# A two-layer graph network in f32 on one core: layer 0's softmax weights built transposed, head pairs in layer 1, and TensorE in the order in which the program is written

## The chip, the core and the metric

The kernel runs on one core of a Trainium2 chip. The metric is the device time in microseconds of one execution. A core has five engines that run their own instruction queues side by side and wait for each other through semaphores: TensorE (PE; its weight loads are shown as PEld), VectorE (DVE), ScalarE (ACT), GpSimd (POOL) and SyncE (SP), which here issues most of the DMA transfers. The matrix products accumulate in PSUM[...]; all other data lies in SBUF.

## What is computed

64 graphs of 256 nodes with 512 features each go through two layers; each ends in a residual and a layer norm. Layer 0 is graph attention, in 8 heads of 64 units: the score of a pair of nodes is a sum of one number of each node. Layer 1 is ordinary attention whose softmax is mixed with the adjacency matrix. With the node mask (here all ones) left out:

```python
# layer 0
feats   = einsum('bnf,hfu->bhnu', X, W)
e_self  = einsum('bhnu,hu->bhn', feats, a_self)
e_neigh = einsum('bhnu,hu->bhn', feats, a_neigh)
dense   = leaky_relu(e_self[..., :, None] + e_neigh[..., None, :], 0.2)
att     = softmax(dense - 1e10 * (1 - A), axis=-1)
x       = layernorm(X + relu(att @ feats + b))
# layer 1
attn    = 0.33 * softmax(q @ k.T / 8) + 0.33 * A + 0.33 * exp(-A)
x       = layernorm(x + (attn @ v) @ W_out + b_out)
```

## The kernel before

The nodes of a graph stand in two row tiles of 128 (`T`), the features in four chunks of 128 (`C`). A loop over the graphs (line numbers are those of the profile) has two halves. In the first, `attend0(b)` (layer 0's attention) is woven with `proj1(b - 1)` (layer 1's projections of the graph before); in the second, `attend1(b - 1)` with `proj0(b + 1)` (layer 0's projections of the next graph). Each of the four returns a list of thunks, and `together` takes them from the two lists by their counts. The order in which each engine gets its instructions is not this order: the Tile framework's scheduler reorders every engine's instructions by readiness and by its own costs, with the order of writing as the priority.

`proj0` transposes x on TensorE, makes the features (`pf`, L237) and both logits (`pe`, L250), and turns the neighbour logits into rows (`pr`). `attend0` spreads the row of one head over all partitions by a matmul (`pd`, L288), takes the leaky relu on ScalarE (`low`, L292) and VectorE (L300), adds the mask on GpSimd (L308), takes the row maximum on VectorE (L134) and the exponential with its sums on ScalarE (L136). The probabilities are then transposed on TensorE (`pp_h`, L148), copied out of PSUM (L152), and multiplied with the features (`av_h`, L159); a division by the sums follows (L314), then bias (L321), relu with the residual (L325) and the layer norm (L203 to L209, with a square root on ScalarE).

`proj1` makes transposed q and k (`pq`, L385), v (`pv`, L399), and the product of the graph matrix with v (`pcv`, L411, after a transpose of that matrix); a product of the mask with itself (`pm`, L353) gives the mask of the scores. `attend1` takes head by head: scores (`pz`, L438, with 64 rows of the array), the mask added on VectorE (L446), and then the same softmax, transpose and product as layer 0, shared in `heads`. After the division the graph part is added on GpSimd (L459), the output is transposed (`pt_o`, L124) and projected (`po`, L472), and residual, norm and store follow.

[...]SP issues the loads of graph b + 2 at the head of each iteration, and the store of out at its end.

Of the kernel before, what the change touches and what calls it, by code (L numbers as in the profile page):

```python
# [16 lines left out]
def kernel(  # L17
# [18 lines left out]
    T = N // P  # row tiles of one graph  # L36
    C = F // P  # chunks of the feature axis
    HG = H // 2  # heads that share one PSUM bank of outputs
    NEG = 1e10  # layer 0: weight of (adj - 1)
    HIDE = 2.0**100  # layer 1: masked scores; any score is absorbed by it  # L40
    LA = 0.33
    L_BOTH = 0.33  # the weight of the adjacency and of exp(-distance)
# [5 lines left out]
    small = ctx.enter_context(tc.tile_pool(name="small", bufs=4))  # L48
    psum = ctx.enter_context(
# [7 lines left out]
    X, ADJ, MASK = {}, {}, {}  # L57

    def load(b):
        X[b] = io.tile([P, T, F], FT, tag="x", name=f"x_{b}", bufs=3)  # L60
        nc.sync.dma_start(X[b], x[b].rearrange("(t p) f -> p t f", p=P))
        ADJ[b] = io.tile([P, T, N], FT, tag="adj", name=f"adj_{b}", bufs=4)
        nc.sync.dma_start(ADJ[b], adj[b].rearrange("(t p) n -> p t n", p=P))
        MASK[b] = io.tile([1, N], U8, tag="mask", name=f"mask_{b}", bufs=4)
        nc.sync.dma_start(MASK[b], nodemask[b : b + 1, :])
# [4 lines left out]
    w0_sb = consts.tile([P, C, H, U], FT, name="w0_sb")  # L70
    for c in range(C):
        nc.sync.dma_start(
            w0_sb[:, c], w0[:, c * P : (c + 1) * P, :].rearrange("h p u -> p h u")
        )
    a_bc = consts.tile([P, 2, H, U], FT, name="a_bc")
# [9 lines left out]
    # q, k and v columns apart, heads side by side  # L85
# [10 lines left out]
    nc.scalar.dma_start(wo_sb, w_out.rearrange("(c p) f -> p c f", p=P))  # L96

    ident = consts.tile([P, P], FT, name="ident")
    make_identity(nc, ident)
    eps = consts.tile([P, 1], FT, name="eps")  # L100
    nc.vector.memset(eps, EPS)
    # sel[k, h, :] is one where k == h: it spreads row h over all partitions
    sel = consts.tile([H, H, P], FT, name="sel")
    nc.vector.tensor_copy(sel, ident[:H, :H].unsqueeze(2).to_broadcast([H, H, P]))

    # wa[f, 0, h] = sum_u w0[h, f, u] a_self[h, u]; wa[f, 1, h] with a_neigh
    wa = consts.tile([P, C, 2, H], FT, name="wa")
    for c in range(C):
        for s in range(2):
            prod = work.tile([P, H, U], FT, tag="o", name=f"prod_{c}_{s}")  # L110
            nc.vector.tensor_mul(prod, w0_sb[:, c], a_bc[:, s])
            nc.vector.tensor_reduce(wa[:, c, s], prod, AX.X, ALU.add)
    # the scale of the scores goes into q's weights (a power of two)
# [4 lines left out]
    def transposed(src, dst, b, what):  # L118
        """dst[:, c, i] = src[i, c-th feature chunk], one thunk per row tile."""
# [9 lines left out]
        return one  # L129

    def softmax_rows(z, p, ssum, h, b, what):
        """p = exp(z - max over j), ssum its sums; z is [i, t, j]."""
        nmax = small.tile([P, T], FT, tag="nmax", name=f"nmax_{what}_{b}_{h}")
        nc.vector.tensor_reduce(nmax, z, AX.X, ALU.max, negate=True)  # L134
        for t in range(T):
            nc.scalar.activation(  # L136
                p[:, t, :],
                z[:, t, :],
                AF.Exp,
                bias=nmax[:, t : t + 1],  # L140
                accum_out=ssum[:, t, h : h + 1],
            )

    def transpose_probs(p, h, b, what, copy):
        pt = ps_tile([P, T, N], "tr", f"pp_{what}_{b}_{h}")
        for j in range(T):
            for t in range(T):
                nc.tensor.transpose(  # L148
                    pt[:, j, t * P : (t + 1) * P], p[:, t, j * P : (j + 1) * P], ident
                )  # L150
        pT = work.tile([P, T, N], FT, tag="pT", name=f"pT_{what}_{b}_{h}", bufs=3)
        copy(pT, pt)  # L152
        return pT

    def probs_values(av, pT, v, h):
        k = h % HG
        for t in range(T):
            for j in range(T):
                nc.tensor.matmul(  # L159
                    av[:, t, k, :],  # L160
                    pT[:, j, t * P : (t + 1) * P],
                    v[:, j, h * U : (h + 1) * U],
                    start=(j == 0),
                    stop=(j == T - 1),
                )

    def heads(scores, v, rec_scale, done, b, what, copy):
        """Thunks: scores of head h, transposes of head h - 2, values of head h - 3."""
        probs, probsT, av = {}, {}, {}
        ssum = small.tile([P, T, H], FT, tag="ssum", name=f"ssum_{what}_{b}", bufs=2)  # L170
        rec = small.tile([P, T, H], FT, tag="rec", name=f"rec_{what}_{b}", bufs=2)

        def step(i):
# [105 lines left out]
    def attend0(b):  # L279
# [4 lines left out]
        def scores(h):  # L284
            if h == 0:
                nc.vector.tensor_scalar_mul(es5, ECOL[b][:, :, :H], 0.2)
# [283 lines left out]
```

## Time and profile before

| | |
|---|---|
| median of 3 runs | 5749.65 us (5746.13 to 5749.77) |
| profiled execution, span from its first to its last instruction | 5748.6 us |
| mean granted TensorE clock | 0.920 |
| busy: PE, PEld, DVE, ACT, POOL | 96%, 67%, 47%, 47%, 23% |
| DMA | 94.69 MB, mean 16 GB/s |

Times are in microseconds unless marked ns. A row of a group names the line, the engine, the operation, what it writes and what it reads, the shape and the count; behind the first bar stand its total busy time and the mean duration of one in ns, behind the second the idle time of the engine ahead of it and what ended it. A row of the timeline has its start, its length, and the instruction with its count. Matmuls are pipelined and their ends are modelled, so what a matmul costs is read from start to next start. A row of the windows has, for a stretch, the busy time and the count of PE, PEld, DVE, ACT and POOL, then the granted clock, the DMA share and GB/s. A row of the DMA list ends with the size of one transfer and its median time from issue to landing.

### The profile page before, as it was taken

The numbers are of one execution on the slowest core, as the hardware profiler recorded it, in microseconds if no ns is written. First come the engines' busy times: TensorE is split into PE (matmuls) and PEld (weight loads), VectorE is DVE, ScalarE is ACT, GpSimd is POOL, SyncE is SP. The second block draws the span as 40 slices with busy tenths as digits, with TensorE's granted clock in tenths as the row PEclk, the third lists the DMA queues.
The fourth block names the chain that finished last, engine by engine and source line by source line (L and its number), as shares of the span: only waits on it lengthen the run. The fifth ranks groups of instructions, "written<-read, shape, count | busy, mean of one in ns | idle before, by whom it ended". The sixth has DMA issues, their size and how long they took to land.

```text
span 5748.6 us, 70111 instructions
## 1 busy us (share of the span) xinstructions
PE 5528.5 (96%) x26240; PEld 3830.8 (67%) x26240; DVE 2687.0 (47%) x5526; ACT 2712.3 (47%) x7104; POOL 1307.0 (23%) x1350
## 2 busy tenths in 40 slices
PE   7999999999999999999999999999999999999999
PEld 5666666666666666666666666666666666666666
DVE  3444544444444444444444444544444445444444
ACT  4444454454444544444445444454454444544543
POOL 2222222122221222222212222222122222222221
PEclk8999999999999999999999999999999999999998
DMA  2000000000000000000000000000000000000000
GB/s 74 15 14 15 17 15 15 14 19 14 15 15 13 19 16 14 16 17 15 15 14 19 15 14 15 17 15 15 14 19 14 16 15 14 18 15 14 12 8 8
DMA packets 70435, 94.69 MB, mean 16 GB/s; under 512 B 19920, under 2 KB 36304, under 8 KB 70096
## 3 DMA queue, kind: packets, MB, share of 16 engines
q1 hardware_dynamic: 56512, 84.96, 4.5%
q10 hardware_dynamic: 13584, 5.24, 0.4%
q8 instruction: 208, 3.41, 0.2%
q14 instruction: 131, 1.07, 0.1%
HBM read 56.64 MB, written 33.55 MB: 16 GB/s over the span
## 4 chain that ended last, share of the span: by engine, by line
PE 91%; ACT 5%; DVE 2%; POOL 1%; issue 1%; DMA 0%; ACTq 0%; SPq 0%; POOLq 0%; DVEq 0%
PE pq L385 19%; PE av_h L159 16%; PE pp_h L148 10%; PE po L472 9%; PE pz L438 8%; PE pf L237 8%; PE pv L399 8%; PE pd L288 5%; PE pcv L411 4%; PE pe L250 2%; ACT low L292 2%; PE pt_o L124 2%; ACT L206 1%; ACT hT L127 1%; DVE z L446 1%; POOL o L459 1%
## 5 line engine op out<-in xcount | busy, mean ns | idle before, releaser
L136 ACT ACTIVATE p_h<-z,nmax_h 128x256 f32<-128x256 f32 x2048 | 1023.3, 501 | 1146.9 <-DVE nmax_h L134 1135.1
L385 PE MATMUL pq<-hT,wqkv_sb 128*128 128x256 f32 x4096 | 1178.8, 438 | 58.0 <-ACT hT L127 58.0
L385 PEld LDWEIGHTS pq<-hT,wqkv_sb 128*128 128x128 f32 x4096 | 868.9, 224 | 195.5 <-ACT hT L127 83.2
L134 DVE TENSOR_REDUCE nmax_h<-z 128x2 f32<-128x512 f32 x1024 | 695.6, 679 | 586.9 <-POOL z L308 584.8
L308 POOL TENSOR_TENSOR z<-z,m 128x512 f32<-128x512 f32 x512 | 648.9, 1268 | 1006.9 <-DVE z L300 821.2
L148 PEld LDWEIGHTS pp_h<-ident,p_h 128*128 128x128 f32 x4096 | 542.3, 156 | 362.4 <-issue 220.3
L148 PE MATMUL pp_h<-ident,p_h 128*128 128x128 f32 x4096 | 749.4, 299 | 1.9 <-ACT p_h L136 1.9
L300 DVE SCALAR_TENSOR_TENSOR z<-pd,ecol,low 128x256 f32<-128x256 f32 x1024 | 455.2, 476 | 424.5 <-ACT low L292 419.5
L159 PEld LDWEIGHTS av_h<-v,pT_h 128*128 128x128 f32 x4096 | 507.8, 194 | 103.5 <-DVE pT_h L152 52.0
L459 POOL TENSOR_TENSOR o<-o,cv 128x256 f32<-128x256 f32 x256 | 180.3, 726 | 1741.0 <-DVE o L452 1741.0
L159 PE MATMUL av_h<-v,pT_h 128*128 128x64 f32 x4096 | 530.5, 274 | 36.0 <-DVE pT_h L152 36.0
L159 PEld LDWEIGHTS av_h<-feat,pT_h 128*128 128x128 f32 x4096 | 513.9, 194 | 55.7 <-issue 30.8
L292 ACT ACTIVATE low<-pd,es 128x256 f32<-128x256 f32 x1024 | 434.1, 469 | 229.7 <-PE pd L288 221.1
L159 PE MATMUL av_h<-feat,pT_h 128*128 128x64 f32 x4096 | 526.7, 272 | 0.0
L438 PE MATMUL pz<-qk 64*128 64x256 f32 x2048 | 510.3, 404 | 13.5 <-DVE z L446 13.5
L472 PE MATMUL po<-wo_sb,oT 128*128 128x512 f32 x1024 | 517.6, 651 | 0.0
L237 PE MATMUL pf<-w_sb,xT 128*128 128x512 f32 x1024 | 499.8, 605 | 0.0
L399 PE MATMUL pv<-wqkv_sb,hT 128*128 128x512 f32 x1024 | 477.6, 599 | 0.0
L152 DVE COPY pT_h<-pp_h 128x512 f32<-128x512 f32 x512 | 351.5, 686 | 245.6 <-PE pp_h L148 240.1
L446 DVE TENSOR_TENSOR z<-pz,hid 128x512 f32<-128x512 f32 x512 | 345.5, 685 | 176.0 <-PE pz L438 169.2
L479 DVE TENSOR_TENSOR x<-po,x 128x512 f32<-128x512 f32 x128 | 88.6, 692 | 718.7 <-PE po L472 718.7
L152 ACT COPY pT_h<-pp_h 128x512 f32<-128x512 f32 x512 | 300.1, 586 | 215.6 <-PE pp_h L148 213.1
(68 smaller groups left out, 5550.0 us busy)
## 6 DMA issues: line engine op xcount, KB each, us to landing
x<-in_x_dram SPq DMA_DIRECT2D x64, 512.0 KB, 3.5
out_dram<-y SPq DMA_DIRECT2D x64, 512.0 KB, 2.8
adj<-in_adj_dram SPq DMA_DIRECT2D x64, 256.0 KB, 2.6
wqkv_sb<-in_L_gnn_W_qkv_dram ACTq DMA_DIRECT2D x12, 256.0 KB, 6.7
mask<-in_nodemask_dram SPq DMA_DIRECT2D x64, 0.2 KB
w_sb<-in_L_gnn_W_dram SPq DMA_DIRECT2D x4, 256.0 KB, 7.3
wo_sb<-in_L_gnn_W_out_dram ACTq DMA_DIRECT2D x1, 1024.0 KB, 7.3
a_bc<-in_L_gnn_a_self_dram ACTq DMA_DIRECT2D x1, 256.0 KB
```

Source lines behind the costliest of these rows:

```text
L134: nc.vector.tensor_reduce(nmax, z, AX.X, ALU.max, negate=True)
L136: nc.scalar.activation(p[:, t, :], z[:, t, :], AF.Exp, bias=nmax[:, t : t + 1], accum_out=ssum[:, t, h : h + 1],)
L148: nc.tensor.transpose(pt[:, j, t * P : (t + 1) * P], p[:, t, j * P : (j + 1) * P], ident)
L152: copy(pT, pt)
L159: nc.tensor.matmul(av[:, t, k, :], pT[:, j, t * P : (t + 1) * P], v[:, j, h * U : (h + 1) * U], start=(j == 0), stop=(j == T - 1),)
L237: nc.tensor.matmul(pf, xT[:, c, t * P : (t + 1) * P], w0_sb[:, c].rearrange("p h u -> p (h u)"), start=(c == 0), stop=(c == C - 1),)
L292: nc.scalar.activation(low[:, t, :], pd, AF.Identity, bias=es5[:, t, h : h + 1], scale=0.2,)
L308: nc.gpsimd.tensor_add(z, z, M0[b])
L385: nc.tensor.matmul(pq[:, s, :], wqkv_sb[:, c, s, 2 * g : 2 * g + 2, :].rearrange("p h u -> p (h u)"), hT[:, c, :], start=(c == 0), stop=(c ...
L399: nc.tensor.matmul(pv, hT[:, c, t * P : (t + 1) * P], wqkv_sb[:, c, 2].rearrange("p h u -> p (h u)"), start=(c == 0), stop=(c == C - 1),)
L438: nc.tensor.matmul(pz[:, t, :], QK[b][r : r + U, g, 0, t * P : (t + 1) * P], QK[b][r : r + U, g, 1, :], start=True, stop=True,)
L472: nc.tensor.matmul(po, oT[:, c, t * P : (t + 1) * P], wo_sb[:, c, :], start=(c == 0), stop=(c == C - 1),)
```

## The change

Layer 0. A head's weights are made with the neighbour on the partitions, so that they can enter the product without a transpose. For this the row maximum is known beforehand: since leaky relu grows with its argument, the largest neighbour logit among the neighbours (`shifts`, 16 fused add-and-minimum reductions on VectorE) gives it. What is then one number per row becomes, transposed, a row for all partitions: `spread` transposes it on TensorE, copies it, writes it to memory (8 KB) and reads it back to all 128 partitions (1 MB). This is done once for the neighbour logits (`rows`) and, after the shifts, twice for the two branches of the leaky relu with the shift taken off (`rows_ab`). `weights(h)` takes the larger branch, adds the transposed mask on GpSimd and takes one exponential; a column of ones in the features gives the sums. The logits are eight extra columns of the features' product.

Layer 1. The masks are made on GpSimd. Two heads are taken together: the scores on the two row halves of the array, and the values, with v as the stationary operand, on two column halves, which gives the output already transposed. The probabilities are divided by their sums, and the graph matrix is added to them, before the transpose; the product of the graph matrix with v goes away.

Both. The root of the norms is a power on GpSimd. `together` weighs thunks by costs, and TensorE's instructions keep the order of writing. ADJ and the mask have three buffers for four.

```diff
+        nc.gpsimd.tensor_scalar_add(rstd, mv[:, :, 1], EPS)
+        nc.gpsimd.tensor_tensor(rstd, rstd, mhalf, op=ALU.pow)
...
+    def spread(cols, k, tag, b, bufs):
+        pr = ps_tile([k, N], "tr", f"pr_{tag}_{b}")
+        for t in range(T):
+            nc.tensor.transpose(pr[:, t * P : (t + 1) * P], cols[:, t, :k], ident)
+        row = small.tile([k, N], FT, tag=f"row_{tag}", name=f"row_{tag}_{b}", bufs=1)
+        nc.vector.tensor_copy(row, pr)
+        there = dram.tile([k, N], FT, tag=f"there_{tag}", name=f"there_{tag}_{b}")
+        nc.sync.dma_start(there, row)
+        bc = work.tile([P, k, N], FT, tag=f"bc_{tag}", name=f"bc_{tag}_{b}", bufs=bufs)
+        nc.sync.dma_start(bc, there[:, :].partition_broadcast(P))
+        return bc
...
+        def features(t, g):
+            pf = ps_tile([P, W1], "mm", f"pf_{b}_{t}_{g}")
...
+            nc.vector.tensor_copy(ECOL[b][:, t, g, :], pf[:, HG * U :])
+            nc.scalar.copy(
+                feat(b)[:, t, g * HG : (g + 1) * HG, :U],
+                pf[:, : HG * U].rearrange("p (h u) -> p h u", u=U),
+            )
         def rows():
+            n_bc[0] = spread(ECOL[b][:, :, 1, :], H, "n", b, 1)
+        def shifts():
+            nmax = small.tile([P, T, H], FT, tag="nmax", name=f"nmax_{b}", bufs=2)
+            for h in range(H):
+                for t in range(T):
+                    junk = work.tile([P, N], FT, tag="junk", name=f"junk_{b}_{h}_{t}")
+                    nc.vector.tensor_tensor_reduce(
+                        out=junk,
+                        in0=n_bc[0][:, h, :],
+                        in1=m0[:, t, :],
+                        scale=-1.0,
+                        scalar=3.0e38,
+                        op0=ALU.add,
+                        op1=ALU.min,
+                        accum_out=nmax[:, t, h : h + 1],
+                    )
...
+        def rows_ab():
+            for g in range(2):
+                ABC[b, g] = spread(
+                    AB[b][:, :, g].rearrange("p t s h -> p t (s h)"), H, "ab", b, 3
+                )
         return [
+            (0.0, bias),
+            *transposed(X[b], xT, b, "x"),
+            *((1.77, lambda t=t: features(t, 1)) for t in range(T)),
+            (0.22, rows),
+            *((1.77, lambda t=t: features(t, 0)) for t in range(T)),
+            (0.44, bias_T),
+            (0.0, shifts),
+            (0.22, rows_ab),
         ]
...
+        def weights(h):
+            g, k = divmod(h, HG)
+            z = work.tile([P, T, N], FT, tag="z", name=f"z0_{b}_{h}", bufs=4)
             for t in range(T):
                 nc.scalar.activation(
+                    z[:, t, :],
+                    ABC[b, g][:, HG + k, :],
                     AF.Identity,
+                    bias=N5[b][:, t, h : h + 1],
                 )
             for t in range(T):
                 nc.vector.scalar_tensor_tensor(
                     z[:, t, :],
+                    ABC[b, g][:, k, :],
+                    ECOL[b][:, t, 1, h : h + 1],
+                    z[:, t, :],
                     op0=ALU.add,
                     op1=ALU.max,
                 )
+            nc.gpsimd.tensor_add(z, z, M0T[b])
+            nc.scalar.activation(z, z, AF.Exp)
+            E[h] = z
+        def values(h):
+            g, k = divmod(h, HG)
             for t in range(T):
+                if k == 0:
+                    av[g, t] = ps_tile([P, HG, U + 1], "av", f"av0_{b}_{g}_{t}")
+                for j in range(T):
+                    nc.tensor.matmul(
+                        av[g, t][:, k, :],
+                        E[h][:, j, t * P : (t + 1) * P],
+                        feat(b)[:, j, h, :],
...
+        def step(i):
+            if i < H:
+                weights(i)
+            if 0 <= i - 2 < H:
+                values(i - 2)
+        return [
+            (0.9 if i >= 2 else 0.0, lambda i=i: step(i)) for i in range(H + 2)
+        ] + [(0.0, end)]
...
+            *transposed(X1[b], hT, b, "h"),
+            (0.0, masks),
+            *((3.46, lambda g=g: qk(g)) for g in range(G)),
+            *((3.43, lambda t=t: values(t)) for t in range(T)),
...
+        def scores(g):
+            pz = [ps_tile([P, T, N], "sc", f"pz_{b}_{g}_{r}") for r in range(2)]
+            for t in range(T):
+                for r in range(2):
+                    rows = slice(r * U, (r + 1) * U)
+                    nc.tensor.matmul(
+                        pz[r][:, t, :],
+                        QK[b][rows, g, 0, t * P : (t + 1) * P],
+                        QK[b][rows, g, 1, :],
...
+            for r in range(2):
+                h = 2 * g + r
+                z = work.tile([P, T, N], FT, tag="p", name=f"p_{b}_{h}", bufs=5)
+                for t in range(T):
+                    nc.vector.tensor_tensor_reduce(
+                        out=z[:, t, :],
+                        in0=pz[r][:, t, :],
+                        in1=HID[b][:, t, :],
...
+            nc.vector.reciprocal(rec[:, :, s], ssum[:, :, s])
...
+                    nc.vector.scalar_tensor_tensor(
+                        probs[h][:, t, :],
+                        probs[h][:, t, :],
+                        rec[:, t, h : h + 1],
+                        CM[b][:, t, :],
+                        op0=ALU.mult,
+                        op1=ALU.add,
+                    )
...
+        def values(g):
+            if g % 2 == 0:
+                av[g // 2] = ps_tile([P, 2, N], "av", f"av1_{b}_{g}")
+            o = av[g // 2]
+            for j in range(T):
+                for r in range(2):
+                    h = 2 * g + r
+                    nc.tensor.matmul(
+                        o[r * U : (r + 1) * U, g % 2, :],
+                        V[b][:, j, h * U : (h + 1) * U],
+                        probsT[h][:, j, :],
...
+        steps = [(0.0, residual)]
+        for i in range(G + 2):
+            if i < G:
+                steps.append((1.2, lambda i=i: scores(i)))
+            if 0 <= i - 1 < G:
+                steps.append((0.9, lambda i=i: flip(i - 1)))
+            if 0 <= i - 2 < G:
+                steps.append((1.2, lambda i=i: values(i - 2)))
         return [
             *steps,
+            *((3.43, lambda t=t: project(t)) for t in range(T)),
+            (0.0, end),
         ]
...
     def together(one, two):
+        total = [max(sum(c for c, _ in x), 1e-6) for x in (one, two)]
+        done = [0.0, 0.0]
         i = j = 0
+        while i < len(one) or j < len(two):
+            first = j >= len(two) or (
+                i < len(one) and done[0] / total[0] <= done[1] / total[1]
+            )
...
+    with tc.manual_schedule(engines={mybir.EngineType.PE}):
```

## The prediction

> **What bounds the kernel now.** I read the page first: busy shares, the chain that ended last, the costliest groups.
>
> ```profile
> PE 5528.5 (96%) x26240; PEld 3830.8 (67%) x26240; DVE 2687.0 (47%) x5526; ACT 2712.3 (47%) x7104; POOL 1307.0 (23%) x1350
> ...
> PE 91%; ACT 5%; DVE 2%; POOL 1%; issue 1%; DMA 0%; ACTq 0%; SPq 0%; POOLq 0%; DVEq 0%
> ```
>
> TensorE carries 91% of the chain; the others are half idle. So I took TensorE's timeline in one middle graph and read what each piece costs from start to next start, not from its busy time, since matmuls overlap.
>
> ```profile
> 2504.84 3.67 PE L385 MATMUL pq<-hT,wqkv_sb 128*128 128x256 f32 x16
> 2508.44 0.69 PE L288 MATMUL pd<-erow,sel 8*128 8x256 f32 x2
> 2509.06 0.66 PE L148 MATMUL pp_h<-ident,p_h 128*128 128x128 f32 x4
> 2509.56 1.00 PE L159 MATMUL av_h<-feat,pT_h 128*128 128x64 f32 x8
> 2510.40 3.67 PE L385 MATMUL pq<-hT,wqkv_sb 128*128 128x256 f32 x16
> ...
> 2530.35 1.14 PE L438 MATMUL pz<-qk 64*128 64x256 f32 x8
> 2531.42 0.66 PE L124 MATMUL pt_x<-ident,x 128*128 128x128 f32 x4
> ...
> 2538.16 1.13 PE L438 MATMUL pz<-qk 64*128 64x256 f32 x4
> 2539.22 1.10 PE L159 MATMUL av_h<-v,pT_h 128*128 128x64 f32 x8
> ```
>
> An f32 matmul stands as two records, a transpose as one. Prices: eight matmuls of q and k 3.60, one spread of a logit row (pd) 0.62, four transposes 0.50, one head's values 0.84, one head's scores 1.06. Two heads that came together (x8) took 1.07: they lie on the two row halves and ran at once.
>
> Last, the windows view around the end of a graph (the column before the DMA share is the granted clock):
>
> ```profile
> 2555.00:2560.00 5.00, 3.47 (x17) 2.67 (x18) 1.45 (x4) 1.16 (x2) 1.40 (x2) 0.75 0.01 3
> 2570.00:2575.00 5.00, 4.50 (x20) 2.46 (x18) 3.02 (x6) 3.72 (x8) 3.12 (x3) 0.95 0.00 0
> 2575.00:2580.00 5.00, 4.56 (x10) 3.02 (x10) 3.52 (x8) 3.49 (x8) 2.20 (x3) 0.50 0.27 104
> 2580.00:2585.00 5.00, 5.00 (x17) 3.92 (x17) 2.56 (x6) 2.55 (x8) 1.55 (x2) 0.52 0.00 1
> 2585.00:2590.00 5.00, 5.00 (x33) 4.32 (x32) 1.76 (x4) 4.79 (x14) 2.21 (x2) 1.00 0.00 0
> ```
>
> About a microsecond of idle TensorE is followed by some ten microseconds at half clock. A graph takes 88.75 us (this pattern returns every 88.75); 13.65 of them are at half clock, which costs 6.8.
>
> [...](only 1.00 and 0.50 granted, in stretches of 3.41 and 10.24 us). [...]this trace has no accumulating VectorE instruction.
>
> **The change part by part: TensorE's work.** Per graph it removes 8 pd (5.0), layer 0's 8 transposed probabilities (4.0), pe (1.9), the mask product (1.1), the transposed graph matrix (0.4), rest (3.6), the transposed output (0.9), half of the scores (3.6) and, if column halves run at once, 3.0 of layer 1's values: 4 matmuls of 256 columns by pairs, 0.93 instead of 2x0.84. It adds transposes of the bias and of the rows (1.0) and eight extra columns in the features (264 for 256: 0.4). Net 22 us. What is left is 29.0 in the half with layer 0's attention (8x0.84 values, 0.95 transposes, 4x3.6 q and k, 2x3.5 v) and 28.3 in the other. If nothing waited this alone would give some 67 us a graph.
>
> **The new wait.** TensorE now runs in emission order, and `together` puts the steps of cost zero first: `step(0)`, `step(1)`, `step(2)` of `attend0` come before any thunk of `proj1`. So the first matmul of this half is `values(0)`, and all of q, k and v queue behind it. It needs this graph's weights, these need ABC, ABC needs two DMAs, the shifts, N broadcast by two DMAs, and `rows`. By the same costs `rows` lies behind `flip(3)`, and `rows_ab` is the last TensorE thunk of its half. This is one closed chain from one graph to the next. Its links:
>
> (a) From `values(0)` to the first scores of layer 1: 29.0 of matmuls, 0.94 for the copy of hT (q's wait in the profile before), 0.8 for the two av buffers between heads 3 and 4 (reciprocal and multiply of the first), 4.3 for about 8.5 us at half clock after the idle (the 10.24 above[...]). 35.0.
>
> (b) From there to the end of `flip(3)`. VectorE sets this. The rows I use (by shape):
>
> ```profile
> L300 DVE SCALAR_TENSOR_TENSOR z<-pd,ecol,low 128x256 f32<-128x256 f32 x1024 | 455.2, 476 | 424.5 <-ACT low L292 419.5
> L325 DVE SCALAR_TENSOR_TENSOR o<-o,x 128x512 f32<-128x512 f32 x128 | 115.0, 937 | 32.7 <-POOL o L321 32.7
> L314 DVE TENSOR_TENSOR o<-av_h,rec_h 128x256 f32<-128x256 f32 x256 | 102.0, 420 | 590.8 <-PE av_h L159 590.8
> ```
>
> Back to back they follow each other 0.08 us sooner. A pair has four reductions from PSUM (0.34 as L314 and 0.08 for the accumulator, 0.42; bounds 0.34 and 0.55), a reciprocal 0.1, four multiply-adds of the graph matrix (0.36): 3.2, four pairs 12.9. Ahead of them stand layer 0's last division 1.0 and its norm 4.4 (2x0.94, 2x0.63, 2x0.15, 2x0.49). Start 1.2, exponentials not covered in the first and last pair 2.0, the last flip 0.95, half clock on TensorE's own share 1.5. Sum 24.0; TensorE's own work up to here is only 14.6 (scores 4.3, x transposes 0.95, two features 3.6, flips 3.8, two values 2.0).
>
> (c) N: transposes 0.2, copy 0.4 (L265's 0.402), two issues 0.35 each, 0.5 of semaphores, and two transfers. From the page:
>
> ```profile
> x<-in_x_dram SPq DMA_DIRECT2D x64, 512.0 KB, 3.5
> out_dram<-y SPq DMA_DIRECT2D x64, 512.0 KB, 2.8
> adj<-in_adj_dram SPq DMA_DIRECT2D x64, 256.0 KB, 2.6
> ```
>
> 256 KB more cost 0.9, so 1 MB of broadcast rows takes an estimated 5.3 (up to wo_sb's 7.3 in the crowded start); 8 KB to memory between 1.7 (the loads' part without size) and 2.8, say 2.2. Sum 9.3. TensorE has 12.8 us of other work beside this and (d): features, values, projection.
>
> (d) Shifts: 16 reductions with both inputs in SBUF, at 0.48 (0.36 if the accumulator is free[...]), 7.7; seven small ones 0.8; a projection's add 0.6. Sum 9.1. So TensorE idles 5.6 here.
>
> (e) ABC, as (c) with the store of out beside it: 9.5. (f) First weights: two identities 0.86, last max 0.45, GpSimd's add 1.27, exponential 0.63, semaphores 0.4: 3.6. TensorE idles through both.
>
> Sum 35.0+24.0+9.3+9.1+9.5+3.6 = 90.5 a graph against 88.75. Start to the first `values(0)`: about 72 (first scores stood at 46; rows at 41, then c to f). Behind the last one: 35+34+23+36. So 72+128+63x90.5 = 5902 us against the profiled span of 5748.6, which is 1 us from the median 5749.65.
>
> **At no cost, and under what.** Layer 1's masks move to GpSimd (about 4.4 us a graph): they need only inputs and run in the idle of (e); without that idle they would stand 4.4 us ahead of (f)'s add. The norm's root leaves ScalarE with its table loads (L206 x128 and L136 x127, four of 1.28 us a graph): ScalarE is no bound, and GpSimd's two tiny operations sit inside the norm, which nothing in TensorE's order waits for until the next graph. Copies move to ScalarE (about 38 us in 90). ADJ's third buffer holds SP's loads until the masks are done, early in the half and ahead of the spreads. If column halves do not run at once, 3.7 us come back, half of them in (b) under VectorE, half beside (c): nothing.
>
> **Rivals.** *Rows come early (faster).* If VectorE does the layer 0 norm after the pairs and the pairs keep TensorE's pace, (b) falls towards 14.6, a graph to 81.1, the kernel to 5310. For it: VectorE had only 47%. Against it: the norm is emitted first, and (b) is VectorE work almost end to end. It decides where (b) falls below 21.6 (2.4 us less). *Reductions at half rate (slower).* Shifts at 0.68 add 3.2, layer 1's at 0.55 add 2.1: 95.8 a graph, 6235; with TensorE at half clock throughout (b) another 6, 6610. For it: the idle that brings half clock is now everywhere. *TensorE stays the bound.* 67 us a graph, 4400: only if `values(0)` did not wait, which the order rules out.
>
> **How the numbers follow.** Main case 0.46 (5800 to 6190), slower rival 0.19, rows early and other savings in the chain 0.31, TensorE bound 0.01, and 0.03 that they cancel. A measurement of this kernel can tell about 0.2% from no change. Faster takes the 0.32 of the third and fourth; same 0.03; slower 0.65. I cut 0.1 off each end: at 5350 (81.7 a graph, (b) near 15) and at 6400 (98.4).
>
> **What would show it.** In the profile after: TensorE near 65% busy; before layer 0's first values of each graph an idle of 12 us or more, released by ScalarE's exponential; a second one before the ab transposes, released by VectorE; mean clock below 0.85; pz rows as x8 in about 1.1; the chain split among TensorE, VectorE and DMA. Wrong if TensorE is above 80% busy, if ABC lands within 5 us of its transposes, or if another queue (SP's store ahead of a spread) holds the chain.

## The result and the profile after

| | before | after |
|---|---|---|
| median | 5749.71 us (4 runs) | 5815.17 us (5814.18 to 5818.96, 4 runs) |
| ratio to before, 95% interval | | 1.0115 [1.0101, 1.0129] |
| profiled span | 5748.6 us | 5812.4 us |
| mean granted TensorE clock | 0.920 | 0.829 |
| busy PE, DVE, ACT, POOL | 96%, 47%, 47%, 23% | 74%, 46%, 37%, 26% |

The change made the kernel 65 us slower, 1.15%. One run among the experiments below (the kernel before in the written order) was slow, 7027 us at a granted clock of 0.784 where the other three took 6475 to 6480 at 0.85, and is left out of that kernel's figures. TensorE's busy time fell by 1213 us, from 5528.5 to 4315.4, and the time rose all the same. The page of the kernel after says where to look: three quarters busy, and a clock line (tenths of full speed in 40 slices) with no slice at full speed.

```profile
PE 4315.4 (74%) x20098; PEld 3048.7 (52%) x20098; DVE 2657.5 (46%) x8864; ACT 2145.9 (37%) x5249; POOL 1504.6 (26%) x1672
...
PEclk7888888888888888888888888888888888888888
```

The chain view of the page breaks off after 1% of the span, so it cannot be set against the 91% that it gave TensorE before. The waits stand in for it: engine, line, what it waited for, the total, the times, the longest.

```profile
ACT z L313 <- DMA bc_ab<-there_ab: 730.9, 64, 15.7
...
PE av L338 <- ACT z L329: 696.0, 65, 11.8
...
PE pz L463 <- DVE nmax L475: 284.9, 127, 4.2
PE pr_ab L188 <- DVE ab L272: 250.2, 64, 9.2
```

Once a graph, TensorE waits 10.7 us for layer 0's first weights and 3.9 us for the shifts; the second pair's scores wait twice for VectorE. Before, no wait of TensorE came to more than 71 us in all. TensorE's timeline in one graph shows the same in its order (start, length, instruction, idle before it and who ended it):

```profile
2506.71 0.46 PE L188 MATMUL pr_n<-ident,ecol 128*8 128x128 f32 x2
...
2524.81 1.02 PE L188 MATMUL pr_ab<-ident,ab 128*8 128x128 f32 x4 [3.08 <-DVE ab L272]
2537.05 1.97 PE L338 MATMUL av<-feat,z 128*128 128x65 f32 x8 [11.23 <-ACT z L329]
...
2541.85 6.67 PE L415 MATMUL pq<-hT,wqkv_sb 128*128 128x256 f32 x16 [1.13 <-ACT hT L160]
...
2572.73 1.14 PE L463 MATMUL pz<-qk 64*128 64x256 f32 x8
...
2578.04 0.73 PE L463 MATMUL pz<-qk 64*128 64x256 f32 x2 [3.14 <-DVE nmax L475]
2580.54 2.07 PE L463 MATMUL pz<-qk 64*128 64x256 f32 x6 [1.78 <-DVE nmax L475]
...
2598.21 0.38 PE L188 MATMUL pr_n<-ident,ecol 128*8 128x128 f32 x2
```

The 16 records of q and k, 3.67 long at full clock, are 6.67 long after the long idle. The windows view (busy time of PE, PEld, DVE, ACT and POOL, then clock, DMA share, GB/s) has the idle, and the half clock that outlasts it into the stretch in which TensorE is busy again:

```profile
2525.00:2530.00 5.00, 0.82 (x4) 0.22 (x2) 1.73 (x4) 0.00 (x0) 0.72 (x1) 0.50 0.42 136
2530.00:2535.00 5.00, 0.00 (x0) 0.00 (x0) 1.07 (x3) 1.61 (x4) 0.10 (x1) 0.50 0.65 236
...
2540.00:2545.00 5.00, 3.87 (x12) 2.85 (x11) 2.38 (x4) 2.82 (x6) 4.20 (x4) 0.50 0.00 0
2545.00:2550.00 5.00, 5.00 (x22) 4.30 (x21) 0.01 (x1) 1.76 (x4) 0.94 (x1) 0.71 0.00 0
```

The transfer inside that idle, from the timeline of all engines: the copied row, SP's issue of the write, the store of out between the two, the read back, and ScalarE released by the landing.

```profile
2526.29 0.41 DVE L190 COPY row_ab<-pr_ab 8x256 f32<-8x256 f32 x1
...
2526.72 0.29 SPq L192 DMA_DIRECT2D there_ab<-row_ab  x1
2527.18 0.51 SPq L559 DMA_DIRECT2D out_dram<-x  x1
2528.57 0.32 SPq L194 DMA_DIRECT2D bc_ab<-there_ab  x1
...
2533.39 2.10 ACT L313 ACTIVATE z<-bc_ab,n 128x256 f32<-128x256 f32 x5 [11.04 <-DMA bc_ab<-there_ab]
```

I measured the links of the predicted chain graph by graph, from the start of one named instruction to that of the next, and took means; N is the broadcast of the neighbour logits, ABC that of the two branches.

| link, us a graph | predicted | after |
|---|---|---|
| (a) `values(0)` to the first scores of layer 1 | 35.0 | 34.59 |
| (b) first scores to `rows` | 24.0 | 25.63 |
| (c) `rows` to the first shift reduction | 9.3 | 9.57 |
| (d) reductions, and the rest up to the ab transposes | 9.1 | 6.27 + 1.81 |
| (e), (f) ab transposes to `values(0)` | 13.1 | 11.83 |
| sum | 90.5 | 89.70 |

In (d), 6.27 runs from the first reduction to the last, with one add of the output projection (0.69) among them; 1.81 is the rest. (e), from the ab transposes to ScalarE's first use of ABC, is 8.19; (f), from there to `values(0)`, is 3.66.

### The profile page after: what moved, and what is told of

Its sections match the earlier page's. It is cut to its first block, busy times and chain, and to the rows that moved or that the text cites. A ratio compares the mean times of both kernels' runs of the same rounds, so it can differ in the third digit from the quotient of the medians.

```text
span 5812.4 us, 59273 instructions
## 1 busy us (share of the span) xinstructions
PE 4315.4 (74%) x20098; PEld 3048.7 (52%) x20098; DVE 2657.5 (46%) x8864; ACT 2145.9 (37%) x5249; POOL 1504.6 (26%) x1672
## 5 line engine op out<-in xcount | busy, mean ns | idle before, releaser
L320 DVE SCALAR_TENSOR_TENSOR z<-bc_ab,ecol,z 128x256 f32<-128x256 f32 x1024 | 686.0, 715 | 1023.4 <-ACT z L313 1023.4
L338 PE MATMUL av<-feat,z 128*128 128x65 f32 x4096 | 585.5, 291 | 741.7 <-ACT z L329 696.0
L338 PEld LDWEIGHTS av<-feat,z 128*128 128x128 f32 x4096 | 584.3, 210 | 852.2 <-ACT z L329 728.6
L328 POOL TENSOR_TENSOR z<-z,m0T 128x512 f32<-128x512 f32 x512 | 681.9, 1332 | 1130.9 <-DVE z L320 1130.9
L313 ACT ACTIVATE z<-bc_ab,n 128x256 f32<-128x256 f32 x1024 | 461.2, 497 | 786.4 <-DMA bc_ab<-there_ab 730.9
L486 ACT ACTIVATE p<-p,nmax 128x256 f32<-128x256 f32 x1024 | 508.5, 498 | 380.4 <-DVE nmax L475 380.4
L229 PE MATMUL pf<-w_sb,xT 128*128 128x264 f32 x2048 | 633.8, 463 | 11.7 <-ACT xT L160 10.1
L229 PEld LDWEIGHTS pf<-w_sb,xT 128*128 128x128 f32 x2048 | 451.3, 229 | 189.5 <-issue 93.9
L501 DVE SCALAR_TENSOR_TENSOR p<-p,rec,cmat 128x256 f32<-128x256 f32 x1024 | 428.1, 480 | 9.0
L475 DVE CUSTOM_DVE_ANT_0 p<-pz,hid 128x256 f32<-128x256 f32 x1024 | 377.2, 415 | 30.4 <-PE pz L463 30.3
L251 DVE CUSTOM_DVE_ANT_0 junk<-bc_n,m 128x256 f32<-128x256 f32 x1024 | 367.7, 421 | 42.2 <-DMA bc_n<-there_n 42.2
```

The source lines that it names most:

```text
L229: nc.tensor.matmul(pf, xT[:, c, t * P : (t + 1) * P], w0_sb[:, c, g], start=(c == 0), stop=(c == C - 1),)
L313: nc.scalar.activation(z[:, t, :], ABC[b, g][:, HG + k, :], AF.Identity, bias=N5[b][:, t, h : h + 1],)
L320: nc.vector.scalar_tensor_tensor(z[:, t, :], ABC[b, g][:, k, :], ECOL[b][:, t, 1, h : h + 1], z[:, t, :], op0=ALU.add, op1=ALU.max,)
L328: nc.gpsimd.tensor_add(z, z, M0T[b])
L338: nc.tensor.matmul(av[g, t][:, k, :], E[h][:, j, t * P : (t + 1) * P], feat(b)[:, j, h, :], start=(j == 0), stop=(j == T - 1),)
L486: nc.scalar.activation(z[:, t, :], z[:, t, :], AF.Exp, bias=nmax[:, t, h : h + 1], scale=-1.0, accum_out=ssum[:, t, h : h + 1],)
```

## The experiments

Each of the twelve kernels was run beside the kernel before, and the ratios are to that. My theory: the time of the kernel after is a closed chain from one graph's `values(0)` to the next, which exists because TensorE keeps the order of writing; what is taken out of a link comes out of the time, and what is taken off TensorE elsewhere does not. The rival: TensorE's own work, or VectorE's new reductions, bind, and the order is a side matter.

### q and k ahead of layer 0's values

```diff
-            together(attend0(b) ..., proj1(b - 1) ...)
+            one = attend0(b) if b < NB else []
+            two = proj1(b - 1) if b >= 1 else []
+            if one and two:
+                for _, thunk in one[:2] + two[:5]:
+                    thunk()
+                one, two = one[2:], two[5:]
+            together(one, two)
```

> Only the order of writing is changed: the transposes of h and the first two q and k products of layer 1 are written ahead of the first values of layer 0. Theory (one closed chain, TensorE waits 11 us behind values(0) for ABC and the first weights): about 9.3 us of work fill that wait and some 3 us of half clock go with it, so about 12 us a graph less than the changed kernel, near 5050 us. Rival (another engine or the pairs of layer 1 set the pace, and the wait only moves): less than 3 us a graph, 5630 or more.

Measured: 5317.47 us, ratio 0.9242 [0.9227, 0.9257]. TensorE's timeline of this kernel:

```profile
2561.48 0.62 PE L188 MATMUL pr_ab<-ident,ab 128*8 128x128 f32 x4 [4.07 <-DVE ab L272]
...
2567.01 9.81 PE L415 MATMUL pq<-hT,wqkv_sb 128*128 128x256 f32 x32 [0.68 <-ACT hT L160]
2577.55 1.11 PE L338 MATMUL av<-feat,z 128*128 128x65 f32 x8 [0.73 <-ACT z L329]
```

Two of the four q and k groups now run while ABC travels, and the wait for the first weights shrinks from 11.23 to 0.73. Nothing but the order in which the thunks are called was touched. The gain is 498 us where I expected about 765. Link (a) gave what it should, 34.6 to 23.0, but (e) and (f) grew from 11.8 to 16.0: the moved matmuls begin at half clock (32 records in 9.81; at full clock 7.2), because the 4.07 us of idle ahead of the ab transposes is still there. They hold the first weights too, through ScalarE: in its queue the copy of the first q and k group stands ahead of them.

```profile
2573.40 0.59 ACT L424 COPY qk<-pq 128x512 f32<-128x512 f32 x1 [6.44 <-PE pq L415]
2573.88 2.10 ACT L313 ACTIVATE z<-bc_ab,n 128x256 f32<-128x256 f32 x5
```

### The planner's order on TensorE

```diff
-    with tc.manual_schedule(engines={mybir.EngineType.PE}):
+    if True:
```

> The block that keeps TensorE in the order of writing is taken away; the planner orders TensorE again as it did in the kernel before. Theory: the planner lets q and k pass the waiting values, so the wait for ABC is covered and the kernel takes 4900 to 5350 us. Rival (the planner's order costs more than the wait): 5815 us or more.

Measured: 5152.02 us, ratio 0.8955 [0.8941, 0.8968]. Everything else of the change is in this kernel, so all else together makes the old kernel 10.4% faster, and the written order then adds 12.9% (5815.17 / 5152.02 = 1.129). TensorE is busy for longer here than in the kernel after (4403.5 us for 4315.4) and the time is 663 us less, so it is not TensorE's work that sets the time there. My theory was too strong, though: the chain does not exist by the written order alone. In the planner's order TensorE still waits for the shifts (6.00 us below), and the links are 21.1, 25.3, 8.4, 8.3 and 15.9. What the written order adds stands in (a), 13.5 us, of which (e) and (f) give back 4. In its timeline q and k stand ahead of the values too, and the first of these waits for nothing:

```profile
2553.25 1.02 PE L188 MATMUL pr_ab<-ident,ab 128*8 128x128 f32 x4 [6.00 <-DVE ab L272]
...
2558.93 10.25 PE L415 MATMUL pq<-hT,wqkv_sb 128*128 128x256 f32 x38 [0.68 <-ACT hT L160]
2569.02 1.00 PE L338 MATMUL av<-feat,z 128*128 128x65 f32 x8
```

### The kernel before in the written order

```diff
+    with tc.manual_schedule(engines={mybir.EngineType.PE}):
-    if NB > 1:
-        load(1)
+        if NB > 1:
+            load(1)
...
```

> The kernel before, with nothing changed but that TensorE keeps the order of writing. It tells whether this order costs the same on any kernel or only meets the new chain of transfers. Theory: before, a head's scores stand two heads ahead of its transposes and no transfer lies between one TensorE step and the next, but the steps of cost zero do not exist and the two lists alternate; the softmax chain of two heads (about 10 us) is covered by some 8 to 9 us of TensorE, so a little is lost at each head: 5800 to 6200. Rival: order costs it as much as it costs the kernel after (5815 against 5152, a factor of 1.129): near 6490. Second rival: nothing, within 20 us of 5750.

Measured: 6475.90 us, ratio 1.1260 [1.1242, 1.1279]. My own theory for this run (5800 to 6200) fell; the rival, that the order costs the same factor on both kernels, holds: 1.126 here, 1.129 there. So the four kernels make a table in which the two parts of the change are nearly independent factors:

| | planner's order | written order |
|---|---|---|
| old computation | 5749.7 | 6475.9 |
| new computation | 5152.0 | 5815.2 |

Down a column the new computation is worth 0.896 and 0.898. This kernel has no transfer in its chain; what TensorE waits for is in its waits view:

```profile
PE pp_h L148 <- ACT p_h L136: 300.3, 196, 3.3
```

before, the same line stood at 1.9 us in all. The span grew by 724 us, TensorE's busy time by 488 (5528.5 to 6016.9, for the same 26240 instructions): the same instructions at a lower clock (0.851 for 0.920) are two thirds of the loss, idle time is one third. The work did not grow. At half clock a record of q and k followed the one before it by 427 ns, at full clock by 216 (medians in the kernel before), so I count half of the busy time that falls into half clock as stretching; without it the busy time is 5114 us before and 5134 here. That the price is the same in both kernels is measured; why two different chains should come to the same factor I can't say, and it may be chance.

### Rows early

```diff
-            *((1.77, lambda t=t: features(t, 1)) for t in range(T)),
-            (0.22, rows),
+            (1.77, lambda: features(0, 1)),
+            (0.3, lambda: features(1, 1)),
+            (1.69, rows),
```

The changed costs put `rows` between `scores(3)` and `flip(2)`, two flips earlier.

> The neighbour rows are transposed and sent right after scores(3) instead of after flip(3), by two changed costs. Theory: N lands some 8 us sooner, the idle of 3.1 us ahead of the ab transposes goes, nothing else: about 190 us less, near 5620 us. Rival (VectorE is full in this half, so sooner reductions push the pairs back by their 6.3 us): 5815 to 6000 us.

Measured: 5606.81 us, ratio 0.9746 [0.9732, 0.9761], 208 us less than after. In its timeline the wait for the shifts ahead of the ab transposes is gone; the wait for the first weights is not:

```profile
2519.95 0.38 PE L188 MATMUL pr_ab<-ident,ab 128*8 128x128 f32 x2
...
2533.24 1.97 PE L339 MATMUL av<-feat,z 128*128 128x65 f32 x8 [12.06 <-ACT z L330]
```

Link (b) falls by 5.4 and (c) by 1.4, but (d) grows by 1.8 and (e), (f) by 1.6. In (d) it is now TensorE that comes last: it is busy for 93% of the time between the rows and the ab transposes (79% in the kernel after), and the shifts are ready 0.95 us before it. In (e) SP's queue costs time: the store of out stands between the write of the first ab row and its read back, waits for layer 1's norm, and the read back goes out 3.47 us after the write, where it took 1.35. 3.3 a graph remain, the amount expected.

### Layer 0's norm behind the pairs

```diff
+            one = attend0(b) if b < NB else []
-            together(attend0(b) ..., proj1(b - 1) ...)
+            together(one[:-1], proj1(b - 1) if b >= 1 else [])
             together(attend1(b - 1) ..., proj0(b + 1) ...)
+            for _, thunk in one[-1:]:
+                thunk()
```

> The end of layer 0 (relu, residual, layer norm: 4.4 us of VectorE) is written after layer 1's half instead of ahead of it; nothing else. Theory (VectorE sets the stretch from the first scores to flip(3), 25.6 us, and the norm stands in it): the stretch falls to about 21, the norm moves into the wait for N, a graph is 4.4 us shorter, near 5540 us. Rival (the pairs' own chain of scores, reduction, exponential and scaling sets it): 5780 to 5815 us.

Measured: 5545.25 us, ratio 0.9640 [0.9625, 0.9654]. Link (b) fell from 25.63 to 21.25, by 4.38, and the other links stayed within 0.4. The prediction had put this norm at 4.4 at the head of (b). The second pair's scores, which waited 3.14 and 1.78 us, wait once in this kernel's timeline:

```profile
2541.37 1.82 PE L463 MATMUL pz<-qk 64*128 64x256 f32 x8 [1.23 <-DVE nmax L475]
```

TensorE's instructions stand in the same order as in the kernel after, so it is the norm on VectorE that (b) waited for.

### The ABC broadcast twice

```diff
         nc.sync.dma_start(bc, there[:, :].partition_broadcast(P))
+        if tag == "ab":
+            nc.sync.dma_start(bc, there[:, :].partition_broadcast(P))
```

> The broadcast of the ab rows is read from memory twice, the second time behind the first; nothing else. Theory (ABC's landing is on the closed chain): a graph is longer by the time of one more 1 MB broadcast, some 4.3 us, so near 6080 us. Rival (the transfer is hidden): unchanged, 5815 us.

Measured: 6084.26 us, ratio 1.0573 [1.0557, 1.0589]. A transfer that was hidden would have cost nothing; it costs 269 us, 4.2 a graph, and link (e), (f) grows by 4.6, from 11.83 to 16.43. So the transfer is not hidden: ABC's landing lies on the chain.

### q and k first, and rows early

The edits of the first and the fourth kernel together.

> The two changes of order that each shortened the changed kernel together: the transposes of h and two q and k products ahead of the first values, and the rows behind scores(3). Theory (two separate links of one chain): the gains add, 5317 less some 205, near 5110 us. Rival (after the first change another resource bounds the kernel): 5280 or more.

Measured: 4830.68 us, ratio 0.8402 [0.8389, 0.8415]. The sum of the two gains would have been 706 us; it is 984. The timeline shows from where the rest comes:

```profile
2556.57 0.60 PE L219 MATMUL pm<-ident,m 128*128 128x128 f32 x4
2557.01 0.38 PE L188 MATMUL pr_ab<-ident,ab 128*8 128x128 f32 x2
...
2560.68 7.17 PE L416 MATMUL pq<-hT,wqkv_sb 128*128 128x256 f32 x32 [0.68 <-ACT hT L160]
2568.59 1.11 PE L339 MATMUL av<-feat,z 128*128 128x65 f32 x8 [0.73 <-ACT z L330]
```

With the rows early no idle stands ahead of the ab transposes, so the q and k that follow run at full clock: 7.17 for the 32 records that took 9.81, and (e), (f) come to 11.6 where the first edit alone had 16.0. Each edit alone leaves one of two idle stretches, and half clock follows either: in the first edit's timeline 4.07 us of idle and then 9.81 for those 32 records, in the second's 12.06 of idle and then 5.39 for 16 records that take 3.67 at full clock. The store of out, which cost the second edit time, stands behind the read back of the first ab row in this kernel.

### The two heads' values one after the other

```diff
-            for j in range(T):
-                for r in range(2):
+            for r in range(2):
+                for j in range(T):
```

> In layer 1's values the two heads of a pair are written one after the other instead of alternately, so that the column halves of the array overlap at most at the seam; nothing else. Theory (this work lies under VectorE's pairs and beside the wait for N): up to 3.7 us more TensorE work a graph, no more than 30 us in the kernel, 5815 to 5845 us. Rival (TensorE's work counts in full): near 6000 us.

Measured: 5820.61 us, ratio 1.0113 [1.0098, 1.0128]. I meant to take away the overlap of the two column halves, and did not: a pair's eight records still take 1.02 us up to the next matmul. The run says only that the order of the four matmuls does not matter. Its timeline:

```profile
2506.87 1.09 PE L533 MATMUL av<-pT,v 128*64 128x256 f32 x8
2507.89 2.05 PE L229 MATMUL pf<-w_sb,xT 128*128 128x264 f32 x8
```

### Both heads on one column half

```diff
-                        o[r * U : (r + 1) * U, g % 2, :],
+                        o[(g % 2) * U : (g % 2 + 1) * U, r, :],
```

on top of the edit before.

> The two heads of a pair are multiplied one after the other, as in the run with the values apart, and both now on the same column half of the array (an even pair on the lower one, an odd pair on the upper one), so that no two heads of a pair can run at once. The output stands permuted, so heads 1 and 2 of every four meet each other's rows of the projection; the amount of work is the same. The theory that the two column halves run at once: a pair's eight records take 1.7 to 1.8 us in place of 1.01 (4 matmuls of 256 columns at 0.45), TensorE gets about 3.2 us a graph more, and since all of it lies under VectorE's pairs and beside the broadcast of N, the time stays between 5815 and 5845, as the prediction says. Rival 1: half of it lands on the chain, 1.6 us a graph, near 5920. Rival 2: the records still take 1.01; then it is not the two halves at once that makes them cheap, and the time stays within 5 us of 5820.

Measured: 5846.70 us, ratio 1.0164 [1.0149, 1.0179]. TensorE's timeline of this kernel:

```profile
2514.18 1.94 PE L533 MATMUL av<-pT,v 128*64 128x256 f32 x8
2516.05 2.05 PE L229 MATMUL pf<-w_sb,xT 128*128 128x264 f32 x8
```

Now they take 1.87, where the run before had 1.02, and the eight records of the features behind them take 2.05 in both, so the clock was the same. So the two halves do run at once where both are used, and 3.4 us a graph (4 x 0.85) of added TensorE work cost 26 us over the run before, 0.4 a graph: about seven eighths of it are hidden. The prediction had them at nothing, half under VectorE's pairs and half beside the broadcast of N.

### The planner's order, and rows early

> TensorE ordered by the planner, and the rows written behind scores(3). Theory: the idle of 6 us ahead of the ab transposes in the planner's version goes, so 3 to 6 us a graph less than 5152, 4780 to 4970 us. Rival (the planner had already placed the rows as early as they can go, or VectorE is the bound there): 5100 or more.

Measured: 4958.63 us, ratio 0.8618 [0.8604, 0.8633]. 193 us less than the planner's order alone, nearly what the edit gave in the written order (208). Link (b) falls from 25.3 to 17.0 and the reductions stretch from 7.1 to 11.4, since in VectorE's queue the output projection's add stands among them and waits for TensorE:

```profile
2607.73 0.69 DVE L556 TENSOR_TENSOR x<-po,x 128x512 f32<-128x512 f32 x1 [4.47 <-PE po L549]
```

### The planner's order, rows early, and the norm late

> The planner's order for TensorE, rows early, and layer 0's norm written behind the pairs. Without the last edit 4959. If the norm's place is set by where it is written, some 3 to 4 us a graph go from the stretch between the scores and the rows: near 4740 (4700 to 4800). Rival: the planner moves VectorE's work by readiness, so the norm was not ahead of the pairs anyway, or the values wait behind the reductions: 4950 or more.

Measured: 4630.63 us, ratio 0.8051 [0.8037, 0.8064], the fastest of all and 110 us below what I expected. Link (b) went from 17.0 to 15.6 and the reductions from 11.4 to 7.9. Here layer 0's norm has become TensorE's longest wait in total, once a graph, as its waits view shows:

```profile
PE pt_h L157 <- DVE x L175: 221.1, 64, 6.2
PE pr_ab L188 <- DVE ab L272: 163.9, 64, 10.0
```

### All three edits in the written order

q and k first, rows early, norm late.

> Three edits together: q and k ahead of layer 0's values, rows early, and layer 0's norm behind the pairs. With the first two 4831. The third alone took 4.4 us a graph away. If it does so here too, 4550; but with rows early the scores to rows link is 20.4 and TensorE's own work in it about 15 to 16, so that part of it may meet TensorE: I expect near 4600 (4550 to 4680). Rival: TensorE, then at 4118 us of busy time, has become the bound in this half, and nothing is gained: 4800 or more.

Measured: 4900.87 us, ratio 0.8491 [0.8436, 0.8547]; one of the four runs took 4831.81 at a clock of 0.925, the others 4900 to 4903 at 0.905, and I don't know why. My expectation (4600) fell: the norm's 4.4 us left link (b), 20.4 to 16.0, and came back in (e), (f), 11.6 to 19.2. The rival had the right size for a wrong reason, since TensorE is busy 86% of the span and waits, as its timeline shows:

```profile
2579.45 0.38 PE L188 MATMUL pr_ab<-ident,ab 128*8 128x128 f32 x2 [0.47 <-ACT m0T L224]
2585.17 1.94 PE L157 MATMUL pt_h<-ident,x 128*128 128x128 f32 x8 [5.33 <-DVE x L175]
```

The transposes of h, which the first edit had pulled to the head of the half, need the norm that the third edit had pushed back. Two moves that pay alone meet in one wait, and the half clock after it (the 32 records of q and k took 10.17 behind such a wait, for 7.17 at full clock).

## Why the prediction was right in its sign and wrong in its size

Predicted: 5900 us, measured 5815, inside the range. The direction and the mechanism held; the change of +150 us is more than twice the measured +65.

**The new wait: right.** `values(0)` stands first in TensorE's order and q, k and v queue behind it: 11.23 us of idle, released by ScalarE's exponential, which waits for ABC. Moving q and k in front of it took 498 us away; doubling the ABC transfer added 269.

**Link (a): right**, 35.0 against 34.59; its 8.5 us at half clock behind `values(0)` are 8.67 on average in the trace of the kernel after. **(b): right in kind**, VectorE's, as the late norm shows; 1.6 too short, and half of that is a wait that the prediction did not count: in layer 0's norm VectorE stands 0.83 us a graph for the root on GpSimd, ahead of reductions for which TensorE waits.

**(c): right in size, in part by luck.** 9.3 against 9.57, but its parts were other ones, and the 0.5 for semaphores, like the 0.4 in (f), was a guess (one hand-over in the kernel before, from ScalarE's copy of hT to q's first matmul, took 0.06). SP's queue holds the read back of N:

```profile
2507.65 0.29 SPq L192 DMA_DIRECT2D there_n<-row_n  x1
2508.92 0.34 SPq L71 DMA_DIRECT2D mask<-in_nodemask_dram  x1
2510.58 0.38 SPq L69 DMA_DIRECT2D adj<-in_adj_dram  x1
2511.06 0.42 SPq L194 DMA_DIRECT2D bc_n<-there_n  x1
...
SPq L69 <- POOL far L391: 84.8, 60, 6.2
```

The last line is of SP's waits. The loads of a later graph wait for the buffers that GpSimd's masks release, and the read back goes out 3.45 us after the write; with the rows early, where no load stands between the two, it takes 1.34. And the transfer is not the only thing that sets this link: in VectorE's queue the add of the output projection stands ahead of the first reduction, and after it VectorE waited for N in 39 of 64 graphs only, 42.2 us in all. So an earlier N would be worth 0.7 us a graph at most while that add stands there (an estimate from the 42.2; no run tried it).

**(d) too long.** I took 0.48 us for a reduction with both inputs in SBUF, an estimate above its lower bound of 0.36. Sixteen and the projection's add took 6.27 where I had 8.3; the first graph's sixteen, with nothing among them, took 5.61 for 7.7. The rest went the other way, 1.81 for 0.8: two statistics of layer 1's norm, 0.68 each, stand among the small ones in VectorE's queue. The groups by shape show why (one input in PSUM, both in SBUF, the accumulator's read):

```profile
L475 DVE CUSTOM_DVE_ANT_0 p<-pz,hid 128x256 f32<-128x256 f32 x1024 | 377.2, 415 | 30.4 <-PE pz L463 30.3
L251 DVE CUSTOM_DVE_ANT_0 junk<-bc_n,m 128x256 f32<-128x256 f32 x1024 | 367.7, 421 | 42.2 <-DMA bc_n<-there_n 42.2
...
L251 DVE DVE_READ_ACCUMULATOR2_ANT nmax<- 128x1 f32 x1024 | 85.7, 84 | 0.0
```

A reduction follows the one before it by 0.35, so the lower bound was the right one. This refutes the slower rival too: its half rate, 0.68 a reduction, was an assumption that no run shows.

**(e) too long**, 9.5 against 8.19, an estimate made from loads of other sizes; **(f) right**, 3.6 against 3.66.

**The sum: the step that failed.** "72+128+63x90.5" counts 63 equal periods. The first one has no layer 1 beside it and took 49.72; that alone is 40.8 us too much, nearly half of the error. The other 62 took 89.77, not 90.5: 45 us. The first `values(0)` came at 65.1, not 72 (7 us), and behind the last one 132.2 us passed, not 128 (4 the other way). 65.1 + 49.7 + 62 x 89.77 + 132.2 = 5812.7, the span of 5812.4. So the failing terms are the count, which took a first period without layer 1 for a full one, and the period itself, 0.7 us too long because (d) and (e) came to 2.3 less and (b) to 1.6 more; the start adds a little. The new period was forecast 1.75 us above the old one (90.5 against 88.75) and came to 1.02 above it, so an error of 0.8% of a period decides the size of the change.

**At no cost: right** for layer 1's values, where the loss of the column halves cost 26 of some 218 us (64 x 3.4). Of the rest no edit was tried by itself, but the trace speaks against three of them. The root has VectorE wait inside (b), as said. ADJ's third buffer does not hold SP's loads ahead of the spreads but in the middle of one, as said under (c). And the masks did not run in the idle of (e): they run from some 3 us before N's transposes to 4 us behind, and the loads wait for them there.

**What would show it.** The clock fell to 0.829 as said (below 0.85) and the scores of a pair stand as x8 in 1.14. The idle before the first weights was said to be 12 us or more and is 10.7 on average; TensorE was said to be near 65% busy and is at 74%, since its busy time is stretched by the half clock: 1032 us of it fall into half clock, and less half of that it is 3799 us, 65%. Another queue that holds the chain was named as a sign of being wrong; SP's loads ahead of N are one, though a small one. The chain view could not be read.

**Rivals.** *Rows come early* did not happen by itself, but what it says of the chain is true: with the norm and the rows moved, (b) fell to 16.0 and 15.6, near the 14.6 of TensorE's own work, and the kernel became faster than before. *TensorE stays the bound* (67 us a graph) "only if `values(0)` did not wait": the planner's order came to 79.1, and to 70.8 with two edits. What the prediction did not do was to price the written order by itself. It is worth 12.9% of the time, and it hides that the new computation is worth 10.4%.

## What to carry to other kernels

An engine's queue is a promise about order: look at what stands first in it after each long transfer, and count what is queued behind. Do this for every queue, the one that issues the DMA included: here a load that waited for a buffer held the transfer behind it (3.45 us from the write to the read back, 1.34 without a load between). Price a new schedule and a new computation apart, and on the old kernel too; here the computation gave 10% and the schedule took 13%. When a sum over periods decides by one per cent, count the first and the last period singly; and take away idle stretches together, since here one that was left still slowed the work after it (9.81 us for records that take 7.17 at full clock).

## What the runs showed of the hardware that I had not expected

- The fused reduction takes 421 ns for 256 elements with both f32 inputs in SBUF and 415 ns with one in PSUM, so where the second input lay made no difference to speak of; nor did it for a scalar_tensor_tensor without an accumulator (L501, both inputs in SBUF, 480 ns; L300 of the kernel before, one in PSUM, 476). The accumulator's read (84 ns) overlaps: in the first graph sixteen reductions took 5.61 us, 0.35 each.
- The column halves of the array run at once for f32: 1.02 us for four matmuls of 256 columns on both halves, 1.87 on one at the same clock, a factor of 1.83. It did not need the heads to alternate (1.02 with the values apart too); how the array pairs them when they don't stays open.
- A power on GpSimd, of two numbers in each partition, takes 716 ns: the second of these lines of the groups by shape, of the kernel after.

```profile
L320 DVE SCALAR_TENSOR_TENSOR z<-bc_ab,ecol,z 128x256 f32<-128x256 f32 x1024 | 686.0, 715 | 1023.4 <-ACT z L313 1023.4
...
L173 POOL TENSOR_TENSOR rstd_l<-rstd_l,mhalf 128x2 f32<-128x2 f32 x128 | 91.6, 716 | 10.7
```

- In the first line a VectorE operation of 256 elements took 715 ns on average, 470 at the shortest and 1531 at the longest, where L501, the same operation on the same shape, took 475 to 488. The long ones are those beside GpSimd: of the 1024, the 383 with no GpSimd instruction beside them took 472 to 486 ns, the 386 with at least 0.4 us of one took 611 to 1531. The shifts' reductions show the same with the rows early: 411 to 425 ns alone, and 1.25 us on average for the 60, one in nearly every graph, that met GpSimd's addition of the masks. Why, and for which instructions, the runs don't show.
